# The second products of a two-layer graph attention kernel: fifteen products in thirds of the features in place of seven

## The chip, the cores and the metric

The kernel runs on one core of a Trainium2 chip. The metric is the device time of one execution in microseconds, as the median of several runs. One execution was also taken by the hardware profiler; its views are quoted here. The engines are called as in the profile: PE (TensorE, matmuls), PEld (its weight loads, which overlap with PE), DVE (VectorE), ACT (ScalarE), POOL (GpSimd) and SP (SyncE, which here only issues transfers). A letter q behind an engine is its sequencer or queue. Transfers that add to what lies at their destination (accumulating DMAs) are issued on POOL, all others on SP, but for two loads and a store on ACT.

## The reference

A graph attention network of two layers on 512 nodes with 768 features and 16,896 edges, a residual connection and a layer norm:

```python
def gat_layer(x, W, a_s, a_d, b, edge_index, concat):
    n = x.shape[0]
    H, C = a_s.shape
    h = (x @ W).reshape(n, H, C)
    src, dst = (edge_index[0], edge_index[1])
    alpha_s = jnp.einsum('nhc,hc->nh', h, a_s)
    alpha_d = jnp.einsum('nhc,hc->nh', h, a_d)
    e = jax.nn.leaky_relu(alpha_s[src] + alpha_d[dst], NEG_SLOPE)
    m = jax.ops.segment_max(e, dst, num_segments=n)
    e = jnp.exp(e - m[dst])
    denom = jax.ops.segment_sum(e, dst, num_segments=n)
    alpha = e / (denom[dst] + EPS)
    msg = h[src] * alpha[:, :, None]
    out = jax.ops.segment_sum(msg, dst, num_segments=n)
    out = out.reshape(n, H * C) if concat else out.mean(axis=1)
    return out + b
h = gat_layer(x, W1, a_src1, a_dst1, b1, edge_list, concat=True)   # 8 heads of 768
h = jax.nn.elu(h)
out = gat_layer(h, W2, a_src2, a_dst2, b2, edge_list, concat=True) # 1 head of 768
...
x = _layernorm(x + out)
```

The first layer has eight heads. Its output, 512 x 6144, is multiplied by W2 (6144 x 768). The kernel does that head by head: the 512 x 768 result of a head, called g here, times 768 rows of W2 is added to h2 (512 x 768). This is the second product of a head, and there are eight of them.

## The kernel before

The edges are counted once into a dense 512 x 512 matrix, so that attention is dense: scores, a softmax by rows, a matmul. After that start-up the loop over heads h = 0 to 6 runs three stages per head, one after another on TensorE:

- the attention stage, `mixed(h, ...)`: features of head h times its attention weights PT, by seven products in three chunks (line 911), and `elu`, which writes g transposed into `gT`. VectorE also does work from a list `fill` there.
- the second product: g times the 768 rows of W2, added to `h2`.
- the projection of head h + 2 (for h up to 5): x times its 768 columns of W1, into `HS[h + 2]`. Head 2's runs by seven products (`projection`), those of heads 3 to 7 by fifteen (`by_thirds`, line 410).

Head 7's attention and second product stand behind the loop; the second layer's attention and the layer norm follow.

Every large product is done by fewer block products than the plain method. The scheme of seven products cuts both matrices into halves: sums of the left blocks (`left`, line 342, into `gS`), sums of the right blocks (`right`, line 353, into the tiles `w1t2` and `w1t4`), seven products P1 to P7 of 256 nodes x 384 x 384, and sums of the results. `second` (line 445) makes it: each product is done for two groups of 128 nodes (three matmuls of 384 columns each, line 367), and each result is evicted from PSUM on its own, 128 x 384, by VectorE, which adds it to `h2` or to a spare tile `u2` (lines 460 and 462). `u2` collects over all heads what has to be added to several blocks of `h2`; `fold` does so at the end (line 1175). An f32 matmul shows as two records in the profile, so a second product has 84 records.

The scheme of fifteen products cuts the features into thirds of 256: the left matrix into 2 x 3 blocks of 256 x 256, the right one into 3 x 3. One product is four matmuls of 256 columns (line 426, eight records), with both groups of nodes beside each other in one PSUM bank, so that an eviction is 128 x 512 (lines 432 and 434). The products form chains: those of one chain (a, b, x, y, z) add up in one bank, which is evicted after every product, and the next product of the chain waits for that. The sums of the left blocks of x are made once (`x_thirds`); five of them lie in DRAM (`stored`) and come into `gT`, which is free then, before each projection (`reload_x`). The sums of the right blocks of W1 are made for each head: `load_thirds` (line 133) loads six rows of blocks into `w2r` and two loads with accumulations into `w2t1`; `rest` loads one more (P11, line 162) and returns the VectorE sums (line 166).

The order of work is written out by hand: each engine runs its instructions in program order, and waits (semaphores) are put in where data, buffers or earlier writes demand them, for transfers too. So what stands behind a waiting instruction on the same engine or queue waits as well. PSUM has five banks for these products (`mm`).

The weights of W2 stand in tiles w1 (loaded by `load_w2` while the projection runs), those of W1 in tiles w2. Softmax and transposition of the next head (`lift`, `leak`, `rank`, `weigh`, `turn_out`, `turn_in`) are spread over the second product's steps; `turn_out` sends a transposing DMA on SP. `attended` makes the attention vectors of the second layer from rows of W2, with three VectorE instructions per head and loads into `w2t2` and `w2t4`.

Of the kernel before, what the change touches and what calls it, by code (L numbers as in the profile page):

```python
# [37 lines left out]
def gat_pass(  # L38
# [17 lines left out]
    P = 128  # L56
# [47 lines left out]
    def load_w(W, h, slot, m):  # L104
# [6 lines left out]
        if slot == "w2":  # L111
            rows_ = wpool.tile([P, DC, D], F32, name="w2r")
            W[h] = [rows_[:, :HK], rows_[:, HK:], t1]
        else:
            W[h] = [wpool.tile([P, HK, D], F32, name=f"{slot}{r}") for r in range(2)] + [t1]
# [17 lines left out]
    def load_thirds(h):  # L133

        m = w1[:, h * D:(h + 1) * D]

        def part(k, n):
            return m[k * TH:(k + 1) * TH, n * TH:(n + 1) * TH].rearrange("(k p) d -> p k d", p=P)

        def flat(j):  # L140
            return wpool.tile([P, HK, HALF], F32, name=f"w2t{j}").rearrange("p k n -> p (k n)")

        rows_, pair_ = wpool.tile([P, DC, D], F32, name="w2r"), flat(1)
        add = ALU.add
        for k in range(DC):
            nc.sync.dma_start(rows_[:, k, :], m[k * P:(k + 1) * P, :])
            if k == 3:
                nc.gpsimd.dma_start(third(rows_, 1, 1), part(1, 2), accum_op=add)
            if k == 5:
                nc.gpsimd.dma_start(third(rows_, 2, 1), part(0, 1), accum_op=add)  # L150
        for j, (k0, k1, n) in enumerate(((0, 2, 2), (0, 1, 0))):
            nc.sync.dma_start(square(pair_, j), part(k0, n))
            nc.gpsimd.dma_start(square(pair_, j), part(k1, n), accum_op=add)
# [4 lines left out]
        def rest():  # L158
# [4 lines left out]
            nc.gpsimd.dma_start(B_["P11"], part(1, 1), accum_op=add)  # L163

            def op(o, a, b, how):
                return lambda: nc.vector.tensor_tensor(B_[o], B_[a], B_[b], op=how)
            return dict(P6=op("P6", "P14", "P4", ALU.subtract), P4=op("P4", "P13", "P4", add),
                        P2=op("P2", "P12", "P13", ALU.subtract), P10=op("P10", "P5", "P1", add),
                        P0=op("P0", "P12", "P0", add), P1=op("P1", "P6", "P1", add),
                        P3=op("P3", "P10", "P3", ALU.subtract), P7=op("P7", "P6", "P7", add))  # L170
# [17 lines left out]
    W1[0] = [wpool.tile([P, HK, D], F32, name=f"w1{r}") for r in range(2)]  # L188
# [221 lines left out]
    def by_thirds(h, A_, B_):  # L410

        HS[h] = hs = hpool.tile([P, NT, D], F32, name="hs")
        new_alpha(h)
        bank = {}

        def out(o):
            return hs[:, 2 * o[0]:2 * o[0] + 2, o[1] * TH:(o[1] + 1) * TH]

        def step(p, chain, o, how):
            def multiply():  # L420
# [3 lines left out]
                for i in range(2):  # L424
                    for k in range(2):
                        nc.tensor.matmul(bank[chain][:, i * TH:(i + 1) * TH], A_[p][:, k, i * P:(i + 1) * P], B_[p][:, k, :],  # L426
                                         start=first and i == k == 0, stop=k == 1, skip_group_check=True)

            def empty():
                ps = bank[chain].rearrange("p (i n) -> p i n", i=2)  # L430
                if how in (1.0, -1.0):
                    nc.scalar.activation(out(o), ps, AF.Copy, scale=how)  # L432
                else:
                    nc.vector.tensor_tensor(out(o), out(o), ps, op=how)  # L434
            return multiply, empty

        plus, minus = ALU.add, ALU.subtract
        return [step(*a) for a in (
            ("P8", "a", (1, 2), 1.0), ("P13", "x", (1, 2), minus), ("P9", "b", (1, 0), 1.0), ("P2", "y", (0, 0), 1.0),
            ("P4", "x", (1, 0), plus), ("P12", "y", (1, 0), minus), ("P6", "x", (1, 1), 1.0), ("P0", "y", (1, 2), plus),  # L440
# [881 lines left out]
```

## Time and profile before

| | |
|---|---|
| runs, us | 640.83, 640.85, 1348.13; median 640.85 |
| profiled execution, us | 640.9, of it the span 639.0 |
| PE busy, us (share) | 628.0 (98%) |
| DVE busy | 506.7 (79%) |
| ACT busy | 312.9 (49%) |
| POOL busy | 63.6 (10%) |
| moved by DMA | 109.87 MB |
| DMA queue of SP and ACT, share of 16 engines | 41.4% |
| DMA queue of POOL | 20.0% |

Of the runs, two agree within 0.02 us; the third has more than twice their time. In the page a group line names the line of the kernel, the engine, the operation, output and inputs, the shapes, how often it ran (x), its busy time in us, the mean of one in ns, and the idle time of the engine in front of these instructions with what ended it. In views by windows the columns are PE, PEld, DVE, ACT and POOL busy, the granted clock of TensorE (1.00 is full), the share of time that the DMA engines were busy (it can come out a little over 1), and GB/s. In views in order of time a line begins with the start and the length in us.

### The profile page before, as it was taken

To read this page: it belongs to the slowest core of one execution; us is meant where nothing else is said; L and a number is where in the kernel's file an instruction comes from. 1 tells how busy PE (TensorE), PEld (TensorE's weight loads), DVE (VectorE), ACT (ScalarE), POOL (GpSimd) and SP (SyncE) were. 2 spreads that over 40 slices of the span, in tenths; PEclk is the share of its full clock that TensorE was granted. 3 is DMA by queue.
4 is the path that set the end of the run, shared out by engine and by line. 5 is a ranking of instruction groups with operands and counts; after the bars stand their busy time and mean duration, and the time that the engine had idled before them with its cause. 6 is when DMAs were issued, how large, how long until landed. Compare 5 with 4: busy or idle time off the path is not lost.

```text
span 639.0 us, 7642 instructions
## 1 busy us (share of the span) xinstructions
PE 628.0 (98%) x2509; PEld 435.7 (68%) x2509; DVE 506.7 (79%) x1079; ACT 312.9 (49%) x546; POOL 63.6 (10%) x105
## 2 busy tenths in 40 slices
PE   8999999999999999999999999999999999999995
PEld 5555586556757886588857886588757886545553
DVE  8989989797787878678886878678776878676675
ACT  5874775730728145641728145641728045543440
POOL 1300011010300220010300120010300110000000
PEclk9999999999999999999999999999999999999999
DMA  8993488696914977188915976198916991400122
GB/s 296 324 241 90 97 228 279 153 259 206 248 49 115 314 211 188 34 282 209 237 68 140 299 212 176 33 294 215 239 47 151 310 274 33 141 16 2 33 58 77
DMA packets 86844, 109.87 MB, mean 172 GB/s; under 512 B 40150, under 2 KB 67982, under 8 KB 86030
## 3 DMA queue, kind: packets, MB, share of 16 engines
q1 hardware_dynamic: 70590, 87.42, 41.4%
q0 software_dynamic: 15776, 21.30, 20.0%
q10 hardware_dynamic: 432, 0.59, 0.3%
q8 instruction: 22, 0.36, 0.2%
q14 instruction: 24, 0.20, 0.1%
HBM read 95.12 MB, written 2.90 MB: 153 GB/s over the span
## 4 chain that ended last, share of the span: by engine, by line
PE 93%; DVE 4%; DMA 1%; ACT 1%; issue 0%; SPq 0%; DVEq 0%; ACTq 0%
PE mm L367 42%; PE mm L426 20%; PE mm L911 18%; PE mm L857 3%; PE mm L1268 3%; PE held L367 2%; PE tr L681 1%; DMA q<-drow 1%; DVE scr L376 1%; PE bc L234 1%; PE held L547 1%; PE bc L681 1%; DVE w1t L359 0%; ACT os L653 0%; DMA drow<-turned 0%
## 5 line engine op out<-in xcount | busy, mean ns | idle before, releaser
L367 PE MATMUL mm<-w,gT 128*128 128x384 f32 x252 | 83.6, 486 | 0.0
L367 PEld LDWEIGHTS mm<-w,gT 128*128 128x128 f32 x252 | 47.9, 190 | 31.9
L588 ACT ACTIVATE q<-q,nmax 128x512 f32<-128x512 f32 x32 | 23.1, 722 | 91.0 <-DVE nmax L584 91.0
L462 DVE TENSOR_TENSOR h<-h,mm 128x384 f32<-128x384 f32 x72 | 39.2, 551 | 30.6 <-PE mm L367 30.2
L432 ACT ACTIVATE hs<-mm 128x512 f32<-128x512 f32 x30 | 17.9, 597 | 91.3 <-PE mm L426 73.0
L911 PE MATMUL mm<-PT,hs 128*128 128x256 f32 x252 | 61.3, 379 | 0.0
L367 PE MATMUL mm<-w1t,gS 128*128 128x384 f32 x180 | 60.6, 487 | 0.0
L911 PEld LDWEIGHTS mm<-PT,hs 128*128 128x128 f32 x252 | 47.8, 190 | 7.2 <-ACT u L915 0.3
L367 PEld LDWEIGHTS mm<-w1t,gS 128*128 128x128 f32 x180 | 34.1, 190 | 24.0 <-DVE w1t L359 0.5
L434 DVE TENSOR_TENSOR hs<-hs,mm 128x512 f32<-128x512 f32 x45 | 30.8, 685 | 23.0 <-PE mm L426 23.0
L911 PE MATMUL mm<-pS,gS 128*128 128x256 f32 x168 | 43.1, 379 | 0.0
L839 ACT COPY PT<-zr 128x1024 uint16<-128x1024 uint16 x34 | 39.1, 1156 | 1.4 <-DMA zr<-pS 0.8
L426 PE MATMUL mm<-w2r,xT 128*128 128x256 f32 x160 | 37.8, 379 | 0.0
L426 PE MATMUL mm<-w2r,gT 128*128 128x256 f32 x160 | 37.5, 382 | 0.0
L911 PEld LDWEIGHTS mm<-pS,gS 128*128 128x128 f32 x168 | 31.9, 190 | 4.3
L426 PEld LDWEIGHTS mm<-w2r,xT 128*128 128x128 f32 x160 | 30.4, 190 | 5.2
L426 PEld LDWEIGHTS mm<-w2r,gT 128*128 128x128 f32 x160 | 30.0, 190 | 5.8 <-DVE hs L434 1.9
L367 PE MATMUL mm<-w1t,gT 128*128 128x384 f32 x96 | 32.5, 488 | 0.3 <-DVE h L460 0.3
L915 ACT COPY u<-mm 128x256 f32<-128x256 f32 x21 | 7.8, 371 | 46.0 <-PE mm L911 46.0
L655 DVE TENSOR_SCALAR os<-nodes,idx 128x512 bf16<-128x512 f16 x104 | 28.8, 349 | 1.4 <-PE tr L681 1.4
L367 PE MATMUL mm<-w,gS 128*128 128x384 f32 x84 | 28.6, 486 | 0.0
L834 ACT COPY pS<-q 128x1024 uint16<-128x1024 uint16 x26 | 27.1, 1044 | 2.6 <-DVE q L817 2.1
(241 smaller groups left out, 1255.7 us busy)
## 6 DMA issues: line engine op xcount, KB each, us to landing
w2r<-in_L_gnn_W_dram SPq DMA_DIRECT2D x48, 384.0 KB, 9.6
w<-in_L_gnn_W_dram SPq DMA_DIRECT2D x43, 384.0 KB, 11.1
gT<-xd SPq DMA_DIRECT2D x5, 1280.0 KB
w1t<-in_L_gnn_W_dram SPq DMA_DIRECT2D x9, 576.0 KB
w<-in_L_gnn_W_dram POOLq DMA_DIRECT2D x8, 576.0 KB, 8.8
w1t<-in_L_gnn_W_dram POOLq DMA_DIRECT2D x7, 576.0 KB, 9.7
w2t<-in_L_gnn_W_dram SPq DMA_DIRECT2D x15, 256.0 KB, 7.3
w2t<-in_L_gnn_W_dram POOLq DMA_DIRECT2D x15, 256.0 KB, 9.0
```

What stands on the lines that cost most here:

```text
L367: nc.tensor.matmul(ps[:, :HALF], A_[p][:, k, i * P:(i + 1) * P], B_[p][:, k, :], start=start and k == 0, stop=k == HK - 1, skip_group_chec ...
L426: nc.tensor.matmul(bank[chain][:, i * TH:(i + 1) * TH], A_[p][:, k, i * P:(i + 1) * P], B_[p][:, k, :], start=first and i == k == 0, stop= ...
L432: nc.scalar.activation(out(o), ps, AF.Copy, scale=how)
L434: nc.vector.tensor_tensor(out(o), out(o), ps, op=how)
L462: nc.vector.tensor_tensor(a, a, ps, op=ALU.subtract if p == "P7" else ALU.add)
L588: nc.scalar.activation(q, q, AF.Exp, bias=nmax, scale=-1.0, accum_out=dens[t])
L655: nc.vector.tensor_scalar(o, nodes, idx[:, c:c + 1], None, op0=ALU.is_equal)
L834: nc.scalar.copy(apart.rearrange("p (h n) -> p h n", h=2), q.bitcast(U16).rearrange("p (n h) -> p h n", h=2))
L839: nc.scalar.copy(PT.rearrange("p s n -> p (s n)").bitcast(U16).rearrange("p (s n h) -> p s n h", s=NT, h=2)[:, :, t * P:(t + 1) * P, :], p ...
L857: nc.tensor.matmul(ps[:, :N], HS[h][:, s, c * P:(c + 1) * P], PT[:, s, :], start=(s == 0), stop=(s == NT - 1))
L911: nc.tensor.matmul(bank[p][:, :HN], A_[p][:, k, c * P:(c + 1) * P], B_[p][:, k, :], start=over is None and k == 0, stop=k == 1, skip_group ...
L1268: nc.tensor.matmul(ps[:, :cols.stop - cols.start], PT[:, s, t * P:(t + 1) * P], h2[:, s, cols], start=(s == 2), stop=(s == 1))
```

## The change

The second products of heads 0 to 6 go by the scheme of fifteen products. Head 7 keeps `second`. Parts of the diff, shortened:

```diff
-    def load_thirds(h):
-
-        m = w1[:, h * D:(h + 1) * D]
+    CHUNKS = {"w1": ((0, 3), (2, 5), (1, 4)), "w2": ((0, 1), (2, 3), (4, 5))}
+
+    def load_thirds(m, slot):
...
+        def add_up(o, i):
+            nc.gpsimd.dma_start(o, i, accum_op=ALU.add)
...
             nc.sync.dma_start(B_["P11"], part(0, 1))
-            nc.gpsimd.dma_start(B_["P11"], part(1, 1), accum_op=add)
+            if slot == "w1":
+                nc.sync.dma_start(B_["P10"], part(0, 1))
+            add_up(B_["P11"], part(1, 1))
...
+            def by_dma(o, i):
+                return lambda: add_up(B_[o], B_[i])
+            ops = dict(P6=op("P6", "P14", "P4", ALU.subtract), P4=op("P4", "P13", "P4", ALU.add),
+                       P2=op("P2", "P12", "P13", ALU.subtract), P3=op("P3", "P10", "P3", ALU.subtract))
+            if slot == "w1":
+                add_up(B_["P0"], B_["P12"])
+                ops.update(P10=by_dma("P10", "P1"), P1=by_dma("P1", "P6"), P7=by_dma("P7", "P6"))
...
+    STEPS = dict(P8=("a", (1, 2), 1.0), P13=("x", (1, 2), -1.0), P9=("b", (1, 0), 1.0), P2=("y", (0, 0), 1.0),
+                 P4=("x", (1, 0), 1.0), P12=("y", (1, 0), -1.0), P6=("x", (1, 1), 1.0), P0=("y", (1, 2), 1.0),
+                 P1=("z", (0, 1), -1.0), P10=("y", (1, 1), -1.0), P5=("z", (1, 1), 1.0), P14=("x", (0, 1), -1.0),
+                 P11=("y", (0, 1), 1.0), P7=("x", (0, 0), -1.0), P3=("y", (0, 2), -1.0))
...
             def empty():
                 ps = bank[chain].rearrange("p (i n) -> p i n", i=2)
-                if how in (1.0, -1.0):
-                    nc.scalar.activation(out(o), ps, AF.Copy, scale=how)
+                if copied:
+                    nc.scalar.activation(out(o), ps, AF.Copy, scale=sign)
+                elif o in by_dma:
+                    passed.append(passed.pop(0))
+                    part = passed[-1].rearrange("p (i n) -> p i n", i=2)
+                    nc.scalar.activation(part, ps, AF.Copy, scale=sign)
+                    nc.gpsimd.dma_start(out(o), part, accum_op=ALU.add)
                 else:
-                    nc.vector.tensor_tensor(out(o), out(o), ps, op=how)
+                    nc.vector.tensor_tensor(out(o), out(o), ps, op=ALU.add if sign > 0 else ALU.subtract)
             return multiply, empty
...
+    def second_by_thirds(h, A_, B_):
+        return by_thirds(h2, A_, B_, ("P8", "P13", "P2", "P4", "P12", "P9", "P6", "P0", "P1", "P10", "P5", "P14", "P11", "P7", "P3"),
+                         h == 0, ((1, 2), (0, 1), (0, 2)))
...
+    def g_thirds(h):
+
+        a = {(i, k): gT[:, c::HK, i * TH:(i + 1) * TH] for i in range(2) for k, c in enumerate((0, 2, 1))}
...
+        return G, dict(P8=op("P8", a[1, 0], a[1, 2], minus), P13=negative("P13", a[0, 0], a[1, 2]),
+                       P14=negative("P14", a[0, 2], a[1, 2]), P3=op("P3", a[0, 2], a[0, 0], minus),
+                       P12=negative("P12", a[0, 0], a[1, 1]), P9=op("P9", a[1, 0], a[1, 1], minus),
+                       P7=op("P7", a[0, 0], a[0, 1], minus), P1=op("P1", G["P7"], a[0, 2], minus),
+                       P6=op("P6", a[1, 2], G["P1"], minus), P10=op("P10", G["P1"], a[1, 1], minus),
+                       P5=op("P5", G["P9"], G["P6"], minus), P11=op("P11", a[0, 1], a[1, 1], plus))
...
+        plan = {0: of_b("P4") + sum_up("P14") + finish[:1], 1: finish[1:] + sum_up("P12", "P9"), 2: sum_up("P7"),
+                3: sum_up("P1") + at(score, 0), 4: sum_up("P6"), 5: at(scored, 0) + at(score, 1), 6: sum_up("P3"),
+                7: at(scored, 1) + at(score, 2), 8: sum_up("P10", "P5"), 9: at(scored, 2) + at(score, 3),
+                10: sum_up("P11"), 11: at(scored, 3) + of_b("P3")}
+        behind_it = {2: of_b("P10", "P1", "P7")}
...
+        for n, (multiply, empty) in enumerate(pairs):
...
+                multiply()
+            for f in plan.get(n, []):
+                f()
...
+            empty()
+            for f in behind_it.get(n, []):
+                f()
...
+            if n in (7, 9, 11, 13):
+                out_by_dma((n - 7) // 2)
+            if 0 < h and n == 11:
+                reload_x()
+            if 0 < h and n == 12:
+                sums = rest_of_thirds()
+            if n == 14:
+                B2, rest_of_w2 = load_thirds(w2[(h + 1) * D:(h + 2) * D, :], "w1")
+                sums2 = rest_of_w2()
```

In words. The right blocks of W2 are loaded by `load_thirds` into the tiles w1 when the fifteenth product is issued. Their eight sums: P6, P2, P4 and P3 on VectorE (P6 and P2 at the end of the projection, P4 in the attention stage, for head 0 in the second product, P3 in the second product), P0, P10, P1 and P7 by accumulating DMAs from tile to tile. P0's is issued with the loads; those of P10, P1 and P7, in this order, behind the eviction of the third product. The twelve sums of left blocks go on VectorE: P8 and P13 at the end of the attention stage (`ends`, new in `mixed`), the others by the table `plan`, in which n is the number of the product before (from 0). They lie in `gS`, in the features of head h, which are not needed any more, and for P8 and P13 in the tile `absent` (head 0: in `pass_`).

Of the fifteen results, the seven for the thirds (1, 2), (0, 1) and (0, 2) of h2 are copied by ScalarE into one of two halves of a tile `pass_` in turn, and an accumulating DMA adds that half to h2; the other eight are added by VectorE as in the projection. In head 0, whose results are the first, ScalarE copies the first result of each third straight into h2. `u2` is now a part of `pass_` and used by head 7 alone; six of the twelve additions of `fold` are gone, those that stood in front of head 7's second product. The reload of x's sums and the load for P11 of W1 move to the twelfth and thirteenth product, ahead of the end of the stage.

255 lines of the change are left out of this document (122 added, 133 removed).

## The prediction

> **What bounds the kernel now.** I read the page's busy times first, then the chain of waits in order of time, then the windows of one head's stages.
>
> ```profile
> span 639.0 us, 7642 instructions
> PE 628.0 (98%) x2509; PEld 435.7 (68%) x2509; DVE 506.7 (79%) x1079; ACT 312.9 (49%) x546; POOL 63.6 (10%) x105
> ...
> 298.14 18.38 PE mm L911 x84
> 316.52 27.09 PE mm L367 x84
> 343.61 26.15 PE mm L426 x120
> ...
> 316.52:343.61 27.09, 27.09 (x86) 15.96 (x85) 20.83 (x47) 14.47 (x26) 0.00 (x0) 1.00 0.30 92
> ```
>
> TensorE is busy for all but 11 us of 639, so matmul time removed comes off the end and a wait added to TensorE goes onto it. A middle head takes 18.38 + 27.09 + 26.15 us: attention, second product (the stage that changes), next projection. The window row covers the second product of head 3, which begins at 316.52; below T is such a beginning. Its columns are TensorE, weight loads, VectorE, ScalarE and POOL, then clock 1.00 and the DMA engines' share 0.30. The profiled execution took 640.9 us, 1.9 more than its span; the median of the runs is 640.85, so I sum against 640.9.
>
> **The matmuls.** The stage now has 84 matmul records of 384 columns. Afterwards it has 120 of 256, the form that the projection (L426) runs already.
>
> ```profile
> L426 PEld LDWEIGHTS mm<-w2r,gT 128*128 128x128 f32 x160 | 30.0, 190 | 5.8 <-DVE hs L434 1.9
> ...
> 345.18 1.89 PE L426 MATMUL mm<-w2t,xT 128*128 128x256 f32 x8
> 346.90 1.89 PE L426 MATMUL mm<-w2r,xT 128*128 128x256 f32 x8
> ```
>
> The projection's 26.15 us hold 1.9/5 = 0.38 us of waiting for evictions; without it 25.77, or 1.72 us per product, as the two starts show (346.90 - 345.18). The change therefore saves between 27.09 - 26.15 = 0.94 and 27.09 - 25.77 = 1.32 us per head. I take 1.1, seven times: -7.7 us (bounds -6.6 and -9.2). This is the whole gain to be had, 1.2%.
>
> **VectorE and ScalarE.** Rows for the operations that come and go:
>
> ```profile
> L462 DVE TENSOR_TENSOR h<-h,mm 128x384 f32<-128x384 f32 x72 | 39.2, 551 | 30.6 <-PE mm L367 30.2
> L434 DVE TENSOR_TENSOR hs<-hs,mm 128x512 f32<-128x512 f32 x45 | 30.8, 685 | 23.0 <-PE mm L426 23.0
> L347 DVE TENSOR_TENSOR gS<-gT 128x768 f32<-128x768 f32 x8 | 7.7, 957 | 0.3
> L360 DVE TENSOR_TENSOR w1t<-w1t,w 128x1152 f32<-128x1152 f32 x7 | 9.4, 1348 | 0.0
> L166 DVE TENSOR_TENSOR w2r<-w2t,w2r 128x512 f32<-128x512 f32 x25 | 17.1, 683 | 0.0
> L432 ACT ACTIVATE hs<-mm 128x512 f32<-128x512 f32 x30 | 17.9, 597 | 91.3 <-PE mm L426 73.0
> ```
>
> In the stage of heads 1 to 6 VectorE loses 14 evictions of 0.55, 4 sums of 0.96 and one of 1.35 (12.9 us), and gets 8 evictions and 12 sums of 0.69 (13.8). That makes 20.8 + 0.9 = 21.7 us of 25.8: still covered, with 4 us to spare. The sums P8 and P13 move into the end of the attention stage, where they delay the last activation by about 0.6 us; TensorE needs P8 at T and P13 a product later, and both are ready. ScalarE gets 7 copies of 0.60 on 14.47 us: covered. I cost all this at nothing; if that cover goes, it is a few tenths per eviction, which the 0.38 above stands for. The six fewer folds at the tail lie beside a saturated TensorE: nothing.
>
> **The DMA chain, which decides.** After product 3 (P2) the changed kernel queues on POOL, for the weights of products 10, 9 and 14, the accumulations P10 += P1, P1 += P6, P7 += P6. Ahead of them stand the accumulations of products 1 (P8) and 2 (P13) into the same third of h2. So four transfers follow one another: P13's waits for P8's to land, as both add to the same bytes; P10's stands behind P13's on POOL's queue; P1's overwrites what P10's reads, so it waits for that. TensorE wants P1 for product 9, at T + 8 x 1.72 = T + 13.75. How such accumulations behave is to be seen near the start of the kernel, where two run from SBUF to SBUF:
>
> ```profile
> 43.19 0.89 POOL L217 DMA_DIRECT2D w2t<-w2t  x1 [11.34 <-DMA w2t<-in_L_gnn_W_dram]
> 49.95 0.86 POOL L218 DMA_DIRECT2D w2t<-w2t  x1 [5.87 <-DMA w2t<-w2t]
> ...
> DMA to landing us min/median/max: 6.5/7.9/9.4
> DMA to landing us min/median/max: 4.8/7.0/9.3
> ...
> 50.00:56.00 6.00, 6.00 (x38) 3.18 (x36) 5.86 (x22) 1.70 (x4) 0.81 (x1) 1.00 0.51 100
> ```
>
> The second waited 5.87 us on POOL until the first (L217, 6.5 us) had landed, and began 0.26 us after that. It moved 576 KB on otherwise quiet engines (share 0.51 of 6 us, so 3.1 us of transfer) and landed after 4.8: 1.7 us are fixed. The Trainium skill ("DMA: Bandwidth & Descriptors", "Two DMAs through the same engine are not ordered") says the same of dependent transfers, to wait for the first one's completion whatever the queue; the 5.87 us agree.
>
> The new accumulations are of 256 KB in runs of 1 KB. Rows for their price:
>
> ```profile
> q0 software_dynamic: 15776, 21.30, 20.0%
> ...
> L148 POOL DMA_DIRECT2D w2r<-in_L_gnn_W_dram x5: 1188/1197/1198, 162.1 to 449.0; - x5
> ...
> DMA to landing us min/median/max: 4.4/4.6/5.2
> ...
> DMA to landing us min/median/max: 2.7/2.7/2.8
> ...
> 316.52:318.52 2.00, 2.00 (x8) 1.17 (x7) 1.71 (x3) 1.94 (x5) 0.00 (x0) 1.00 1.00 285
> 320.52:322.52 2.00, 2.00 (x8) 1.17 (x7) 2.00 (x4) 0.00 (x0) 0.00 (x0) 1.00 0.82 287
> 324.52:336.52 12.00, 12.00 (x39) 7.10 (x38) 8.68 (x21) 4.53 (x10) 0.00 (x0) 1.00 0.00 0
> ...
> 318.88 0.40 ACT L850 ACTIVATE nl<-nl 128x256 f32<-128x256 f32 x1
> ```
>
> POOL's queue (q0) took 20.0% of 639 us for 21.30 MB: 6.0 us per MB, so 1.6 us for 0.262 MB. With 1.7 fixed and an issue 0.3 longer (1.197 against 0.86) a landing in the quiet stretch takes 3.6 us by estimate. The ends are 2.7 (the transposing transfers of L836, which add nothing) and 4.8 (the quiet 576 KB). While loads still run, to about T + 6 by the shares 1.00 and 0.82, I use the 4.6 of L148, a 256 KB accumulation among loads.
>
> Now the chain. ScalarE ends its activations at 319.28 = T + 2.8; with 0.6 of delay and the copy of 0.6, POOL starts P8's transfer near T + 4.1. It lands at 8.7; P13's starts at 8.95; POOL issues for 1.2, P10's starts at 10.15, lands at 13.75; P1's starts at 14.0, lands at 17.6; TensorE goes on at 17.7. It has waited 4.0 us. With 2.7 for every landing the wait is 0.25, with 4.8 it is 6.55. Heads 1 to 6: 6 x 4.0 = 24 us (bounds 1.5 and 39). P7 lands some 1.2 us after P1 and is wanted five products later: nothing. The results P1, P14 and P11, added to one third of h2 in turn, also wait for each other, but no matmul reads h2: nothing but POOL's time.
>
> Head 0 has no transfer for P8, but its POOL queue is held by the weights of head 2, and the engines are full:
>
> ```profile
> 105.94 1.27 POOL L121 DMA_DIRECT2D w2r<-in_L_gnn_W_dram  x1 [1.63 <-DMA w2r<-in_L_gnn_W_dram]
> ...
> 99.10 7.90 PE L367 MATMUL mm<-w,gT 128*128 128x384 f32 x24
> ...
> 106.00:112.00 6.00, 6.00 (x20) 3.40 (x19) 5.96 (x9) 1.33 (x3) 1.22 (x1) 1.00 1.03 300
> 112.00:118.00 6.00, 5.67 (x18) 3.09 (x17) 5.93 (x14) 3.02 (x7) 0.00 (x0) 1.00 1.12 274
> ...
> DMA to landing us min/median/max: 5.7/8.9/13.7
> ```
>
> POOL comes free at 107.2; P13 issues, P10's starts at 108.4 and at shares over 1 lands in 4.6 (L148) to 13.7 us (the last row, L153, 256 KB accumulations under full load). I take its median 8.9: 117.3; P1's follows at 117.6 and lands in the calmer 3.6 to 4.6 at about 121.5. Product 9 is due at 99.1 + 13.75 = 112.85: 9 us of waiting (bounds 3 and 13).
>
> Other transfers: the project-stage loads of the next w2 rows need some 0.8 MB more, but the reload of gT and one weight third move ahead into the quiet stretch, so nothing gets later there.
>
> Sum: 640.9 - 7.7 + 24 + 9 = 666 us, with the bounds 638 and 685.
>
> **Rivals.** First, the chain lands in time. It needs 4.1 + 3L + 1.2 + 3 x 0.25 below 13.75, so a landing L of at most 2.6 us; then only the saving stays: 640.9 - 7.7 = 633, within 2% and not slower. For it speaks that the engines stand at 0.00 in 324.52 to 336.52; against it that no accumulation in the trace landed under 4.4. The Trainium skill ("DMA: Bandwidth & Descriptors", "Anatomy of one DMA") gives 2.0 us plus bytes over 436 GB/s, which is 2.6 for 256 KB and this rival; for the quiet 576 KB it would give 3.4, where the trace has 4.8. Chance 0.10.
>
> Second, the clock. The stage rows show TensorE busy without a break and the clock at 1.00, so no row excludes that a wait of 4 us lowers it. If one product after each of seven waits ran at half speed, that is 7 x 1.72 = 12 more: 678. The Trainium skill ("TensorE: Matmul & The Clock Gate", "Part 1: The HAM clock gate") has the clock halved after an idle window of about 3.4 us; no run here shows it yet. Chance 0.07.
>
> Third, landings quick enough but VectorE late: sums and evictions in its 21.7 us bunch up and cost 1 us per head, 633 + 7 = 640. Its 4 us of room speak against it. Chance 0.05.
>
> **How the numbers follow.** The forecast, a wait for P1 in every head, has 0.78. The line of 2%, about what a measurement of this kernel can tell from no change, lies at 653.7; it is passed once a head waits over 2.2 us, which a landing of 3.4 us gives. I put 0.56 above it and 0.22 below. With the rivals: slower 0.56 + 0.07, within 0.22 + 0.10 + 0.05 less 0.02, faster 0.02, since the largest saving of 9.2 us is below 2%. The range 640 to 685 leaves out the first rival and the far end of the second.
>
> **What would show it.** Right: TensorE idle before the first matmul of product 9 in each second product, released by a DMA into the w1 rows; POOL's wait before P13's transfer ended by P8's landing; second-product stages of 29 to 31 us, head 0's longer. Wrong: stages near 26 us, landings of 2.6 us, a clock below 1.00, or VectorE as the releaser of TensorE's idle time.

## The result, and the profile after

The changed kernel takes 723.32 us (median of four runs, 717.48 to 728.21) against 640.97 before: a ratio of 1.128, 95% interval 1.115 to 1.141. The profiled execution took 719.5 us, 717.6 of it the span.

The page of the changed kernel, its first lines and POOL's DMA queue (before: 639.0 us, PE 628.0, DVE 506.7, POOL 63.6; q0 21.30 MB, 20.0%):

```profile
span 717.6 us, 8533 instructions
PE 644.5 (90%) x2761; PEld 492.7 (69%) x2761; DVE 515.7 (72%) x1102; ACT 337.4 (47%) x594; POOL 178.0 (25%) x200
...
q0 software_dynamic: 39824, 41.62, 37.8%
```

TensorE now stands idle for 73 us of the span instead of 11. The queue moves 20.3 MB more, and its share grows from 127.8 to 271.3 us of 16 engines: 7.1 us per MB for what came in. The view of waits says for whom TensorE and VectorE stood still; its columns are the waiting engine and line, the releaser, the total in us, how often, and the longest:

```profile
PE mm L448 <- DMA w1r<-w1t: 53.0, 7, 13.3
PE mm L942 <- DVE w L953: 5.7, 3, 4.2
...
DVE w1t L170 <- DMA w1t<-in_L_gnn_W_dram: 11.1, 5, 3.7
```

(Line 367 of before is 380 here, 426 is 448, 434 is 461, 911 is 942.) Seven waits for a transfer into the w1 rows, one per head, are the waits for P1 that the prediction's steps end in. The other two lines belong together: VectorE's sum of P2, at the end of the projection, waits for late rows of W2, and the attention stage then waits for VectorE.

Head 1 in order of time, POOL first, then TensorE. The stage begins at T = 189.22:

```profile
193.55 1.20 POOL L459 DMA_DIRECT2D h<-pass  x1 [8.69 <-ACT pass L458]
198.60 1.19 POOL L459 DMA_DIRECT2D h<-pass  x1 [3.85 <-DMA h<-pass]
199.31 1.71 POOL L144 DMA_DIRECT2D w1t<-w1r  x1
204.34 2.41 POOL L144 DMA_DIRECT2D w1r<-w1t  x2 [3.32 <-DVE q L608]
```
```profile
189.22 1.99 PE L448 MATMUL mm<-w1r,absent 128*128 128x256 f32 x8
...
208.19 3.29 PE L448 MATMUL mm<-w1r,gS 128*128 128x256 f32 x8 [4.89 <-DMA w1r<-w1t]
211.28 2.32 PE L448 MATMUL mm<-w1t,hs 128*128 128x256 f32 x8
...
222.86 1.46 PE L448 MATMUL mm<-w2r,xT 128*128 128x256 f32 x6
```

The four POOL lines are the transfers of P8's result, P13's result, the weights P10 and the weights P1 (with P7). Asked for each transfer alone, the profile gives 4.5, 3.6, 4.5 and 3.8 us from issue to landing. P13's and P1's start some 0.5 us after the landing that they wait for; P10's is issued 0.7 us behind P13's, while that one is under way. (The releaser at 204.34, an operation on q, has nothing to do with w1r; what P1's waits for is P10's transfer, which reads those rows.) TensorE goes on at T + 19.0 after 4.89 us. Then it is slow: the product at 208.19 takes 3.09 us to the next start, where 1.73 is usual. The windows of the same head show both causes; the columns are as before, PEclk third from the end, then the DMA engines' share:

```profile
198.00:200.00 2.00, 2.00 (x11) 1.77 (x10) 1.97 (x4) 0.00 (x0) 1.40 (x2) 1.00 0.00 0
200.00:202.00 2.00, 2.00 (x11) 1.77 (x10) 2.00 (x5) 1.43 (x3) 1.01 (x1) 1.00 0.93 146
202.00:204.00 2.00, 1.30 (x7) 0.80 (x5) 2.00 (x5) 0.00 (x0) 0.00 (x0) 1.00 0.81 116
...
208.00:209.00 1.00, 0.81 (x3) 0.76 (x4) 0.00 (x0) 0.63 (x1) 0.42 (x1) 0.86 1.19 172
209.00:210.00 1.00, 1.00 (x4) 0.73 (x4) 0.00 (x0) 0.00 (x0) 0.00 (x0) 0.50 1.07 152
...
211.00:212.00 1.00, 1.00 (x4) 0.82 (x3) 0.00 (x0) 0.48 (x1) 0.00 (x0) 0.50 1.58 130
212.00:213.00 1.00, 1.00 (x5) 0.81 (x5) 0.00 (x0) 1.00 (x4) 0.59 (x1) 0.93 0.88 85
```

From P13's issue at 198.60 to 200 nothing moves. Then P13's and P10's 256 KB go together and fill all engines for (0.93 + 0.81) x 2 = 3.5 us, 6.6 us per MB. And the clock falls to half behind the wait, for some 3.4 us.

Head 2 (T = 267.49) waits 8.96 us. POOL's transfers there, and two windows:

```profile
271.82 1.19 POOL L459 DMA_DIRECT2D h<-pass  x1 [6.68 <-ACT pass L458]
280.75 1.20 POOL L459 DMA_DIRECT2D h<-pass  x1 [7.74 <-ACT q L604]
281.47 1.70 POOL L144 DMA_DIRECT2D w1t<-w1r  x1
286.50 2.41 POOL L144 DMA_DIRECT2D w1r<-w1t  x2 [3.33 <-DMA w1t<-w1r]
```
```profile
273.50:275.50 2.00, 2.00 (x11) 1.77 (x10) 1.86 (x4) 0.72 (x1) 0.00 (x0) 1.00 1.04 372
275.50:277.50 2.00, 2.00 (x11) 1.76 (x10) 1.63 (x3) 0.00 (x0) 0.00 (x0) 1.00 0.86 198
```

Most of the difference to head 1 is P8's landing: 8.0 us in place of 4.5, with the engines full of loads until T + 10. P13's transfer then starts 0.9 us after it in place of 0.5. (The operation on q that is named as the releaser at 280.75 is a step of the softmax that has no part in P13's result.) P10's and P1's land after 4.5 and 4.0 us, much as before. In heads 3 and 4 P8's took 7.2 and 6.5 us.

The sum of stages, from TensorE's starts: the second products of heads 0 to 6 took 191.5 us before and take 43.50, 33.64, 37.74, 36.84, 36.69, 33.65 and 36.98 = 259.0 now, 67.5 more. The attention stages take 10.6 more, most of it in head 5 (25.73 us against 18.38). There TensorE waits 4.2 us for VectorE, and the clock is at 0.50 behind that wait as well (504 to 508); 1.1 of the 10.6 are head 0's, whose attention stage is as long in every version below, late rows or not. The projections are unchanged.

### The profile page after: what moved, and what is told of

It reads as the page before. It is cut to its first block, busy times and chain, and to the rows that moved or that the text cites. A ratio compares the mean times of both kernels' runs of the same rounds, so it can differ in the third digit from the quotient of the medians.

```text
span 717.6 us, 8533 instructions
## 1 busy us (share of the span) xinstructions
PE 644.5 (90%) x2761; PEld 492.7 (69%) x2761; DVE 515.7 (72%) x1102; ACT 337.4 (47%) x594; POOL 178.0 (25%) x200
## 4 chain that ended last, share of the span: by engine, by line
PE 55%; DMA 19%; DVE 15%; issue 5%; ACT 4%; SPq 1%; POOL 1%; DVEq 0%; POOLq 0%; ACTq 0%
PE mm L448 22%; PE mm L942 13%; PE mm L380 13%; DMA w1t<-in_L_gnn_W_dram 5%; DMA w1r<-w1t 4%; DMA w1r<-in_L_gnn_W_dram 4%; DVE h L461 3%; PE mm L1329 3%; DMA h<-pass 3%; DVE q L608 2%; PE held L380 2%; DVE q L613 2%; DMA gT<-xd 1%; DMA w2t<-in_L_gnn_W_dram 1%; PE tr L710 1%
## 5 line engine op out<-in xcount | busy, mean ns | idle before, releaser
L459 POOL DMA_DIRECT2D h<-pass x46 | 62.3, 1354 | 185.0 <-ACT pass L458 126.3
L448 PE MATMUL mm<-w1r,gS 128*128 128x256 f32 x168 | 52.7, 469 | 53.4 <-DMA w1r<-w1t 53.0
L461 DVE TENSOR_TENSOR h<-h,mm 128x512 f32<-128x512 f32 x53 | 36.3, 685 | 82.7 <-PE mm L448 80.9
L448 PEld LDWEIGHTS mm<-w1r,gS 128*128 128x128 f32 x168 | 37.8, 233 | 65.2 <-DMA w1r<-w1t 55.8
L458 ACT ACTIVATE pass<-mm 128x512 f32<-128x512 f32 x46 | 26.3, 584 | 35.1 <-PE mm L448 29.0
L448 PE MATMUL mm<-w1t,hs 128*128 128x256 f32 x168 | 42.6, 400 | 0.0
L144 POOL DMA_DIRECT2D w1r<-w1t x21 | 25.2, 1358 | 64.5 <-DMA w1t<-in_L_gnn_W_dram 30.2
L448 PE MATMUL mm<-w1r,hs 128*128 128x256 f32 x168 | 39.3, 383 | 1.2 <-ACT pass L458 1.2
L448 PEld LDWEIGHTS mm<-w1t,hs 128*128 128x128 f32 x168 | 35.1, 209 | 6.0
L448 PEld LDWEIGHTS mm<-w1r,hs 128*128 128x128 f32 x168 | 31.3, 190 | 7.5 <-ACT pass L458 3.6
```

The source lines that it names most:

```text
L144: nc.gpsimd.dma_start(o, i, accum_op=ALU.add)
L458: nc.scalar.activation(part, ps, AF.Copy, scale=sign)
L459: nc.gpsimd.dma_start(out(o), part, accum_op=ALU.add)
L461: nc.vector.tensor_tensor(out(o), out(o), ps, op=ALU.add if sign > 0 else ALU.subtract)
```

## The experiments

The time is the median, the ratio is to the kernel before on the same chip, and "second product" is that of a middle head. T, the products and their numbers are those of the prediction.

| | us | ratio, 95% interval | second product |
|---|---|---|---|
| before | 641 | 1 | 27.09 |
| after | 723.3 | 1.115 to 1.141 | 33.6 to 37.7 |
| weight sums on VectorE | 669.6 | 1.039 to 1.047 | 29.2 |
| results on VectorE | 666.8 | 1.039 to 1.043 | 28.3 |
| both on VectorE | 662.4 | 1.032 to 1.036 | 29.2 |
| TensorE kept busy | 716.7 | 1.113 to 1.124 | 31.9 to 37.2 |
| weight transfers first | 698.6 | 1.081 to 1.094 | 28.7 to 33.9 |
| copies first | 653.7 | 1.018 to 1.022 | 28.4 |
| P2's sum later | 714.3 | 1.108 to 1.116 | 32.7 to 38.8 |
| combined | 649.7 | 1.011 to 1.015 | 27.4 |
| no loads | 706.8 | 1.101 to 1.105 | 32.5 to 35.1 |
| P14 for P11 | 694.4 | 1.083 to 1.088 | 35.7 to 36.8 |
| P1 on VectorE | 697.3 | 1.085 to 1.090 | 35.9 to 37.0 |
| two results by DMA | 644.3 | 1.004 to 1.006 | 26.6 |

The theory after the result: the order P8, P13, P10, P1 on POOL and on the DMA engines makes P1 late, the wait lowers the clock, and the transfers make weight rows late. The rivals: VectorE is late, or accumulations are too slow here in whatever order.

**Weight sums on VectorE.** P10, P1 and P7 of W2 are added by VectorE; the results still go by DMA.

```diff
-                nc.sync.dma_start(B_["P10"], part(0, 1))
+                pass
...
-                ops.update(P10=by_dma("P10", "P1"), P1=by_dma("P1", "P6"), P7=by_dma("P7", "P6"))
+                ops.update(P10=op("P10", "P5", "P1", ALU.add), P1=op("P1", "P6", "P1", ALU.add), P7=op("P7", "P6", "P7", ALU.add))
-        behind_it = {2: of_b("P10", "P1", "P7")}
+        behind_it = {2: of_b("P10"), 3: of_b("P1"), 8: of_b("P7")}
```

> The sums P10, P1 and P7 of the weights go on VectorE; the results still go to h2 by DMA. Chain theory (the wait of product 9 for the accumulation chain, 53 us, and the lowered clock behind it, about 20 us, are the loss): no wait of TensorE for the w1 rows, clock 1.00, second products of 26 to 27 us, in all 632 to 645 us. Rival (the transfers into h2 crowd POOL and the DMA engines and are the loss by themselves, here through the late weights of the next stages): second products stay over 30 us or the attention stages grow, in all over 680 us. Rival (VectorE becomes the bound): TensorE waits for VectorE, second products of 28 us or more, 650 us.

669.6 us. No wait for P1 is left, so 54 of the 82 us go with those three transfers. But the time lies between the numbers of the theories, because another wait came: for ScalarE's copy of P0's result, 1.68 us ahead of product 10 in each middle head. From TensorE and ScalarE of head 3:

```profile
351.81 1.99 PE L448 MATMUL mm<-w1t,hs 128*128 128x256 f32 x8 [1.68 <-ACT pass L458]
```
```profile
349.85 0.72 ACT L617 ACTIVATE q<-q,nmax 128x512 f32<-128x512 f32 x1 [2.59 <-DVE nmax L613]
350.48 0.19 ACT L617 ACTIVATION_READ_ACCUMULATOR q<-q,nmax 128x1 f32 x1
350.57 0.71 ACT L604 ACTIVATE q<-q,al_d 128x512 f32<-128x512 f32 x1
351.18 0.57 ACT L458 ACTIVATE pass<-mm 128x512 f32<-128x512 f32 x1
```

The product was done when ScalarE stood waiting for nmax, a softmax step ahead of the copy in its order; so the copy came late, and product 10 adds into the same bank. In the changed kernel the wait for P1 had hidden this.

**Results on VectorE, and both.** All fifteen results are added by VectorE, with the weight sums by DMA as in the change, or on VectorE too.

```diff
-                         h == 0, ((1, 2), (0, 1), (0, 2)))
+                         h == 0, ())
```

> All fifteen results are added to h2 by VectorE (head 0 as changed); P10, P1 and P7 of the weights stay accumulating transfers, with nothing of h2 ahead of them on POOL. Queue theory (the chain is late because it stands behind the two transfers of P8 and P13): P10's transfer starts near T + 6 and P1's lands near T + 15, a wait of 1 to 2 us per head and no lowered clock from it; VectorE has 4 to 5 us more per head, so second products of 27 to 29 us; in all 645 to 660 us. Rival (two dependent accumulations are late wherever they stand, because the loads of the attention stage still hold the engines): waits of 4 us and more stay, over 680 us.

> Neither results nor P10, P1, P7 by DMA: VectorE does it all, P0 alone stays a transfer. VectorE then has some 21.7 + 4.8 + 1.8 = 28.3 us per second product against 25.8 of matmuls. If VectorE is the bound without the transfers, second products take 28 to 30 us, TensorE waits for VectorE, 650 to 665 us. If the evictions fit after all, 26 to 27 us and 632 to 642 us. Either way no wait for w1 rows and a clock of 1.00.

666.8 and 662.4 us; the first is above the 660 expected at most, the second within its range. With the results' transfers away, the wait for P1 is gone in heads 1 to 6 though its transfers are still there; head 0 keeps 8.9 us of it, behind the loads for head 2 (the prediction's 9). All attention stages but head 0's are back at 18.44 to 18.47 us: the late rows were late because of the results' transfers. What limits now is VectorE. The window of head 3's second product, with both on VectorE:

```profile
326.02:355.25 29.23, 26.89 (x122) 22.58 (x121) 27.98 (x61) 15.57 (x26) 0.00 (x0) 1.00 0.32 94
```

VectorE is busy for 27.98 of 29.23 us, so giving results to the DMA was not without a reason. In head 1 its lateness even brought the clock down (the eight records of one product take 3.62 us):

```profile
195.19 3.62 PE L448 MATMUL mm<-w1t,hs 128*128 128x256 f32 x8 [2.18 <-DVE hs L1041]
```

**TensorE kept busy.** Six more matmuls of 512 columns (head 0: twelve), whose result nobody reads, stand ahead of product 9.

```diff
+            if n == 8:
+                dummy = bc.tile([P, 512], F32, name="bc")
+                for _ in range(6 if h else 12):
+                    nc.tensor.matmul(dummy, ident, cnt[:, 0, :], start=True, stop=True)
```

> The changed kernel with 6 matmuls of 512 columns (5.2 us; head 0: 12, 10.4 us), whose results nobody reads, ahead of product 9 of each second product, so that TensorE is not idle for long there. Clock theory (behind each wait the clock is halved for about 3.4 us, which costs 2.6 to 3.8 us in each of seven heads): the wait ends at the same time, the products behind it run at 1.72 us again, granted clock 0.98 to 1.00, in all 695 to 705 us. Rival (the slow products are slow because of the transfers, not the clock): products of 3 us behind the wait stay, 715 to 725 us.

716.7 us, where the rival's number was (715 to 725) and not the theory's (695 to 705); its two runs, 713.8 and 719.5, overlap with those of the changed kernel, so the total decides nothing. The heads do. Heads 1 and 3, with two windows of head 3:

```profile
206.93 1.89 PE L448 MATMUL mm<-w1r,gS 128*128 128x256 f32 x8
...
219.80 1.89 PE L448 MATMUL mm<-w2r,xT 128*128 128x256 f32 x8
...
369.18 2.86 PE L448 MATMUL mm<-w1r,gS 128*128 128x256 f32 x8 [2.76 <-DMA w1r<-w1t]
```
```profile
369.00:370.00 1.00, 0.82 (x4) 0.75 (x5) 0.00 (x0) 0.00 (x0) 0.00 (x0) 1.00 1.27 243
...
371.00:372.00 1.00, 1.00 (x4) 0.82 (x3) 0.00 (x0) 0.00 (x0) 0.00 (x0) 0.50 1.24 197
```

In head 1 the added matmuls fill the wait, and the last seven products take 219.80 - 206.93 = 12.87 us where the changed kernel takes 222.86 - 208.19 = 14.67. So one fallen clock costs 1.8 us. In head 3 a wait of 2.76 us is left, and the clock falls all the same. In sum the second products got 13.0 us shorter, but the attention stages 11.7 longer, since late rows now held them for more (waits for VectorE's line 953: 13.4 us instead of 5.7).

**Weight transfers first.** Only POOL's order changes.

```diff
-        behind_it = {2: of_b("P10", "P1", "P7")}
+        behind_it = {}
+        for f in of_b("P10", "P1", "P7"):
+            f()
```

> Only POOL's order is changed: the transfers of the weight sums P10, P1 and P7 are issued ahead of the second product's loop, so ahead of those of the results P8 and P13; nothing is taken away, all bytes are still moved. Order theory (the weights are late because they stand behind the results on POOL's queue and behind their wait for each other): in heads 1 to 6 P10's transfer starts about 4 us before the stage, P1's lands by T + 10 at the latest, TensorE does not wait for it and its clock stays at 1.00, so a second product takes 26 to 27.5 us; head 0, where loads fill the engines, still waits up to 9. With late loads of the next weight rows left, 650 to 675 us. Rival (crowding: accumulations into and out of SBUF are slow as such, whatever the order): P1 is still late in most heads, stages above 31 us, over 695 us.

698.6 us: a miss for the theory's number. The time, and most stages above 31 us, are what the rival had forecast, but not for its reason: the waits for P1 fell from 53.0 to 14.6 us, 11.7 of them in head 0, where the loads for head 2 still stand ahead. P10's transfer, now among the loads, took 14.1 us from 182.46 to its landing, P1's started at 197.15, and the results queued behind it:

```profile
182.46 2.49 POOL L144 DMA_DIRECT2D w1t<-w1r  x1
197.15 2.41 POOL L144 DMA_DIRECT2D w1r<-w1t  x2 [12.20 <-DVE h L461]
...
209.41 0.60 ACT L458 ACTIVATE pass<-mm 128x512 f32<-128x512 f32 x1 [1.54 <-DMA h<-pass]
```

(The releaser at 197.15, an addition to h2, has no part in P1's weights.) A copy then waits for a half of `pass_` that a transfer still reads; waits for ScalarE's copies add up to 20.4 us (1.2 after). The order decides which transfer is late, but not that one is.

**Copies first.** On the kernel with the weight sums on VectorE, ScalarE's copies for DMA stand ahead of the softmax steps of their place.

```diff
                 multiply()
+            if n in (0, 1, 7, 8, 11, 12):
+                empty()
             for f in plan.get(n, []):
...
-            empty()
+            if n not in (0, 1, 7, 8, 11, 12):
+                empty()
```

> As the kernel with the weight sums P10, P1 and P7 on VectorE (669.6 us), but ScalarE copies a result for DMA ahead of the softmax steps of the same place instead of behind them. If the waits of 1.68 to 3 us before product 10 there come from the place of the copy in ScalarE's order, they go in every head and a second product takes 27 to 28 us in place of 29.2 to 32: 652 to 660 us. If ScalarE is full in that stretch as such, the softmax is late instead and the time stays within 3 us of 669.6. Late loads of weight rows (attention stages of 20 to 25 us) stay in both.

653.7 us, within the expected 652 to 660, but in part by luck. The second product is 28.4 and not under 28, and the late rows, expected to stay, are gone too (18.44 or 18.47 in each attention stage of heads 1 to 6). Of the 19 us between the two profiled executions only some 7 lie in the second products, where they were expected, and 12 in the attention stages. A likely reason is that results sent sooner free POOL's queue for the next rows; it was not tried alone.

**P2's sum later.** VectorE adds P2's weights in the attention stage.

```diff
-                if n in (13, 14):
-                    sums2.pop("P6" if n == 13 else "P2")()
+                if n == 13:
+                    sums2.pop("P6")()
-            behind = [sums2.pop("P4")]
+            behind = [sums2.pop("P2"), sums2.pop("P4")]
```

> Only the place of one sum is changed: VectorE adds P2's weights in the attention stage, beside P4's, and not at the end of the projection, for heads 1 to 6. Theory of late loads: the attention stages of heads 1 to 6 come back to 18.4 to 18.6 us (after: 18.44, 18.47, 18.95, 18.59, 25.73, 20.27), which is 9 us less, so 711 to 716 us; the waits for P1 stay as they are. Rival (what is late is late, the wait for the rows only moves to the second product or to P6's sum): no stage gets shorter in sum, 719 to 724 us.

714.3 us, within the expected 711 to 716. The attention stages of heads 1 to 6 come back to 18.44 us but for one of 19.70, 8.5 us less in all, as forecast. But the waits for P1 total 56.6 us (53.0), the second products got 4.0 us longer, and between the two profiled executions 3.8 us are left; that the medians differ by 9 owes something to the spread of the changed kernel's runs.

**Combined.** Weight sums by DMA as in the change, for head 0 ahead of the loads; only P13's, P0's and P11's results by DMA, copied first; P2's sum later; x's sums reloaded ahead of a transposition.

```diff
-                elif o in by_dma:
+                elif p in by_dma:
-                         h == 0, ((1, 2), (0, 1), (0, 2)))
+                         h == 0, ("P13", "P0", "P11"))
         if h == 0:
+            for p in ("P10", "P1", "P7"):
+                sums2.pop(p)()
             load_w1(2)()
...
+            if n in (1, 7, 12):
+                empty()
```

> All that the other runs point to in one: the weight sums P10, P1 and P7 stay with the DMA but are issued two products earlier (head 0: ahead of the loads for head 2); only the results of products P13, P0 and P11 go by DMA, the other four on VectorE; their copies stand ahead of the softmax steps; P2's weights are added in the attention stage; x's sums are reloaded ahead of a transposition. If the three causes found (POOL's order, results that VectorE or ScalarE gives back late, late weight rows) are all there is, a second product takes 26 to 27.5 us, no attention stage over 18.6, and the time is 634 to 646 us, within 1% of the kernel before. If the transfers crowd each other whatever their order, waits of 1 to 3 us per head are left and it is 650 to 665.

649.7 us, above the expected 646. The weight transfers of heads 1 to 6 stand at the same place in the program as in the change; with P8's result on VectorE one link ahead of them is gone, and P10's starts at T + 5.4 in head 2. Of the 53.0 us of waiting for P1, 1.7 are left. The last product still waits for P11's copy, in each middle head as here:

```profile
275.10 1.99 PE L448 MATMUL mm<-w1r,hs 128*128 128x256 f32 x8 [0.60 <-ACT pass L458]
```

**No loads.** The next head's W1 rows are loaded for head 3 only; heads 4 to 7 are projected with what is left in the tiles.

```diff
-            B3, rest_of_thirds = load_thirds(w1[:, (h + 2) * D:(h + 3) * D], "w2")
+            if h == 1:
+                B3, rest_of_thirds = load_thirds(w1[:, (h + 2) * D:(h + 3) * D], "w2")
```

> Left out: the rows of W1 and the two sums that load_thirds brings in the attention stage are loaded for head 3 alone; heads 4 to 7 are projected with what is left of them, so the engines have little to move in heads 2 to 5 while the second product's first results are sent. If it is the loads that stretch each landing, the chain of four takes 3.6 us a landing there: P8 starts at T + 4.3, P1 lands near T + 16.3, TensorE waits 2 to 3.5 us in heads 2 to 5 (after: 8.96, 8.05, 7.43, 4.91), heads 0, 1 and 6 stay as they are (13.3, 4.9, 5.5), and the late rows of heads 4 and 5 (25.73) are gone: 685 to 700 us. By the price of 2.6 us a landing there would be no wait at all in heads 2 to 5: below 680. If an accumulation of 256 KB is slow as such, landings stay near 5 and the waits at 5 to 7: over 700.

706.8 us, just inside the rival's number, and the waits lie between: 3.98, 4.89, 3.94 and 4.84 us in heads 2 to 5. POOL and TensorE in head 2, T = 268.34:

```profile
272.67 1.19 POOL L459 DMA_DIRECT2D h<-pass  x1 [18.89 <-ACT pass L458]
276.83 1.19 POOL L459 DMA_DIRECT2D h<-pass  x1 [2.97 <-issue]
277.55 1.69 POOL L144 DMA_DIRECT2D w1t<-w1r  x1
282.57 2.41 POOL L144 DMA_DIRECT2D w1r<-w1t  x2 [3.33 <-DVE q L608]
```
```profile
286.40 2.53 PE L448 MATMUL mm<-w1r,gS 128*128 128x256 f32 x8 [3.98 <-DMA w1r<-w1t]
```

So there are two parts. The loads are the difference between 8.96 and 3.98 us in head 2. Without them P8's and P13's transfers land after 3.6 us, just the estimate for quiet engines, but P10's, which starts beside P13's, after 4.5, and P1's after 3.8, with some 0.5 us from a landing to the next start: the chain is too long by itself. The late rows, expected to be gone, are still there (26.29 us in head 6's attention stage), so the loads of W1 cannot be all that makes them late.

**P14 for P11, and P1 on VectorE.** On the combined kernel, P14's result goes by DMA in place of P11's (head 0: neither), and VectorE's attention steps move from products 7 and 13 to 14; in the second kernel P1's weight sum is on VectorE too.

```diff
-                         h == 0, ("P13", "P0", "P11"))
+                         h == 0, ("P13", "P0") if h == 0 else ("P13", "P0", "P14"))
-            for n, f in zip((6, 12, 12), attend):
+            for n, f in zip((13, 13, 13), attend):
```
```diff
-                7: at(scored, 1) + at(score, 2)
+                7: of_b("P1") + at(scored, 1) + at(score, 2)
```

> As the combined kernel (649.65 us), with three places changed: P14's result goes by DMA in place of P11's (head 0: neither), so that the last product, which uses P11's bank, does not wait for a copy behind the softmax on ScalarE; head 0's copy of P1 stands ahead of the softmax; the three instructions of VectorE for the second layer's attention stand two results from the end. If what is left over the floor of 25.8 us is late evictions, a second product takes 26.2 to 26.9 us (combined: 27.44) and head 0's under 28.5 (29.85): 641 to 646 us. If VectorE is simply full, another product waits in its place and the time stays within 2 us of 649.65.

> As the kernel before it in this call, with P1's weight sum on VectorE two products ahead of its use, so that only one transfer is left in the order P10, P1. If the waits of 0.75 and 0.5 us for P1 (heads 1 and 3 of the combined kernel) are what is left of the chain, they go: 0 to 3 us less than the kernel before it in this call, 640 to 645 us. If VectorE waits in line for P10's transfer, results behind it are late and it is slower by 2 us or more.

694.4 and 697.3 us: both 50 us off. VectorE in head 2 of the first:

```profile
287.91 0.69 DVE L461 TENSOR_TENSOR h<-h,mm 128x512 f32<-128x512 f32 x1 [9.01 <-DMA h<-pass]
```

P14's and P11's results go to the same third of h2. With P14's by transfer and P11's on VectorE, VectorE waits 9.0 us for the transfer to land, and the last product 7.5 us for VectorE. In the second kernel no wait for P1 is left, in the first 2.7 us; whether that pays was covered by the error.

**Two results by DMA.** P14's result goes to VectorE as well.

```diff
-                         h == 0, ("P13", "P0") if h == 0 else ("P13", "P0", "P14"))
+                         h == 0, ("P13", "P0"))
```

> As the kernel with P1's weight sum on VectorE (697.27 us), but P14's result is added by VectorE: only P13's and P0's results go by DMA, both to the third (1, 2) of h2, so that VectorE never adds to a third that a transfer still works on. If the 7.5 us of waiting before the last product came from that order on one third alone, they go in heads 1 to 6, a second product takes 26.3 to 27 us, and the time is 638 to 645 us. If VectorE with one result more is late by itself, a product waits 1 us or more in each head: over 648.

644.3 us, as expected, and the best version of the scheme. Windows over head 2's second product:

```profile
247.45:274.05 26.60, 26.44 (x121) 22.69 (x121) 25.70 (x57) 16.23 (x27) 4.83 (x4) 1.00 0.68 158
```

26.60 us is 0.49 less than before's 27.09, at full clock, with VectorE busy for 25.70 of it. Heads 0, 1 and 6 lose more than that (28.55 against 27.79, 27.69 against 27.21, 31.05 against 28.16), and head 0's attention stage another 1.1, so the kernel before, at 641.1 on the same chip, stays 0.5% ahead.

## Why the prediction was right and wrong

The prediction named the direction and the mechanism: TensorE waits for P1 ahead of product 9 in every head, behind P8's and P13's transfers. Its total, 666 us, was 57 short, and its range was left by 38. Term by term, in us, between the two profiled executions, whose spans differ by 78.6:

| term | predicted | measured |
|---|---|---|
| wait for P1, heads 1 to 6 | 24 (1.5 to 39) | 53.0 - 13.3 = 39.7 |
| wait for P1, head 0 | 9 (3 to 13) | 13.3 |
| clock behind the waits | 0 (rival: 12) | about 13.7 |
| attention stages, 9.8 of it late weight rows | 0 | 10.6 |
| second products without waits and clock | -7.7 | 259.0 - 53.0 - 13.7 - 191.5 = +0.8 |
| the rest | 0 | 0.5 |

**The chain: right in kind, short in size.** In head 1 it ran nearly as written: P8's start T + 4.3 (4.1), its landing T + 8.8 (8.7), P10's start T + 10.1 (10.15), P1's T + 15.1 (14.0), TensorE's T + 19.0 (17.7). The price of a landing in quiet engines with no other ahead of it, 3.6 us by estimate, came out to the tenth: P13's in head 1, P8's and P13's in head 2 of the run without loads. The failed step is that P10's landing was given the same 3.6 us, the engines alone, although P13's transfer is issued 0.7 us ahead of it; it took 4.5, without loads too. With it failed the 0.25 us from a landing to the next start, which was 0.5. In heads 2 to 4 another step failed, "While loads still run, to about T + 6", with 4.6 us for P8. That end was read from head 3 of the kernel before; in head 2 of the changed kernel, which moves 20 MB more on the same engines, the loads ran to T + 10 and P8's landing took 8.0 us. It is the added transfers that push the loads back: in the run with both on VectorE, which sends neither results nor these sums by DMA, the engines of head 2 are all but quiet from T + 6 on (share 0.06 in the next 2 us).

**Head 0** was right in cause, and its 13.3 us are just over the far end of 13. POOL's transfers of P10 and of P1 with P7:

```profile
108.47 2.21 POOL L144 DMA_DIRECT2D w1t<-w1r  x1
123.95 2.41 POOL L144 DMA_DIRECT2D w1r<-w1t  x2 [13.27 <-issue]
```

P10's transfer landed after 15.0 us and kept P1's back for 15.5, where the estimate took 8.9 and was bounded by a row of 13.7.

**The clock** was the second rival, "If one product after each of seven waits ran at half speed, that is 7 x 1.72 = 12 more". It happened in each head, and its price was nearly right: 1.8 us per head by the run with TensorE kept busy, and in head 0 15.8 us from product 9 to the end of the stage against 12.87, so 2.9; taking 1.8 for all of heads 1 to 6 gives 6 x 1.8 + 2.9 = 13.7. Wrong was its chance of 0.07: it was made a rival to the wait, though it follows from the wait and belonged into the sum. The Trainium skill ("TensorE: Matmul & The Clock Gate", "Part 1: The HAM clock gate") has the clock go to half after an idle window of about 3.4 us and come back after as long a busy one. The second half agrees with head 1 (below 1.00 for some 3.4 us); in head 0 the clock stayed below 1.00 for some 5.8 us, which is the 2.9 us lost there. For the first half less was enough here: 2.76 us in head 3 of the run with TensorE kept busy, and 2.18 in head 1 of the run with both on VectorE. No sharp limit shows, since a wait of 2.53 us left the clock up in the run with weight transfers first (sixteen records in 3.72 us):

```profile
365.85 3.72 PE L448 MATMUL mm<-w1r,hs 128*128 128x256 f32 x16 [2.53 <-ACT pass L458]
```

**"So nothing gets later there"**, of the loads, was wrong: the late rows cost 10 us, the fall of the clock in head 5 included. The run with P2's sum moved took them off the attention stages (and gave a part back in the second products), and they were gone wherever the results' transfers were away or sent sooner.

**The saving** of 1.1 us per head did not come. With the wait filled, a stage takes 13.92 us for its first eight products and 12.87 for the rest, 26.79, so 0.3 below 27.09: the floor of 25.77 was taken from the projection, whose results VectorE and ScalarE give back on time. Here ScalarE's copies stand behind softmax steps; that this is what the missing 1.0 us went to is likely, but no run shows it alone, and even the best version with its copies first stays at 26.60. VectorE's 21.7 us were counted about 1 short: the window of head 2 has 24.1, of which two sums of 0.69 at its end are the projection's. That cost nothing while P1 was waited for, but the better versions, which give results back to VectorE, use up the room: 25.70 of 26.60 us in the last of them.

**The first rival**, a landing of 2.6 us, estimated from the figures of the Trainium skill ("DMA: Bandwidth & Descriptors", "Anatomy of one DMA"), was rightly held unlikely. All transfers out of `pass_` in the changed kernel:

```profile
DMA to landing us min/median/max: 3.6/5.2/14.3
```

The quickest took 1 us longer than the 2.6 that it needs.

One slip changes nothing: by the prediction's own sum the line of 2%, 653.7 us, is passed at a wait of 1.9 us per head (640.9 - 7.7 + 9 + 6 x 1.9), not at 2.2.

What stays open: the price of a transfer from tile to tile was measured only in this pattern (256 KB in runs of 1 KB), so what of it is the adding and what the short runs was not tried. Of head 6's 2.9 us over the kernel before in the best version, two waits of TensorE make up 2.1: 0.89 us for ScalarE ahead of product 10 and 1.25 for VectorE ahead of product 14; what makes those late was not followed up.

## What to carry to other kernels

A sum that is moved from an idle-looking engine to an accumulating DMA becomes a link in a chain: price it by the landing beside everything else that is in flight, its own neighbours in the chain first, add the half microsecond from a landing to the next start, and list what waits for the same bytes, on VectorE too. If the chain makes TensorE wait for some microseconds, add the clock's fall to that wait as a term of the sum. And an edit that saves 4% of a stage needs all results given back on time: look at each copy's place in its engine's order, not only at the engine's share.

## What the runs showed of the hardware

An accumulating transfer of 256 KB from tile to tile moved nothing for the first 1.4 us, and two of them together filled the engines for 3.5 us (6.6 us per MB). Alone and without loads one landed 3.6 us after its issue, one issued 0.7 us behind another after 4.5, and among loads P8's took up to 8.0 us (head 2) and P10's of head 0 15.0. Idle stretches of 2.76 and, once, 2.18 us brought TensorE's clock to 0.50, while one of 2.53 and all of 1.68 us left the products behind them at their usual speed. VectorE's addition to a third of h2 on which a transfer was under way stood 9.0 us behind it, by the wait that the kernel sets there.
